# A two-layer state-space and expert kernel: the norm of the chunk two ahead begun in round 17 for 20, x loaded in six pieces, idle products at the start, first repeats in another order, and the last image's normalised tiles kept on chip

## The chip, the cores and the metric

The kernel runs on one core of one Trainium2 chip. The metric is the device time of one execution in microseconds (us). It was taken in five runs; one further view is a profile of one of these executions, from which every row below comes. The engines are named as the profile names them: PE (TensorE, matmuls; PEld is its weight loads), DVE (VectorE), ACT (ScalarE), POOL (GpSimd) and SP (SyncE, which issues nearly all DMAs). All arithmetic is in 32-bit floats, for which the profile records two passes for each matmul instruction.

## The reference

`x` has 8 images of 384 channels and 32 x 32 points, which are 1024 tokens an image. Two layers follow one another, each of the form `x = x + layer(group_norm(x))` with 32 groups that span a whole image.

```
# layer 0: a state-space block and an MLP
t = layernorm(tokens(gn(x))) * ln_w + ln_b
xm, z = split(t @ in_proj.T)                     # 768 + 768
xc = silu(causal_conv3(xm) + conv_b)
dt, B, C = split(xc @ x_proj.T)                  # 24, 16, 16
dt = softplus(dt @ dt_proj.T + dt_b)
h[l] = exp(dt[l]*A) * h[l-1] + dt[l]*xc[l]*B[l]  # 768 channels x 16 states, over 1024 tokens
y = (sum over states of h[l]*C[l] + xc*D) * silu(z)
t = y @ out_proj.T
x = x + gelu(t @ mlp_w1.T + b1) @ mlp_w2.T + b2
# layer 1: four experts, all computed, weighted
g = gn(x); scores = softmax(g @ gate_w + gate_b); the top 2 of 4 give coefficients
x = x + sum over e of coef[e] * (relu(g @ w1[e].T + b1[e]) @ w2[e].T + b2[e])
```

The coefficients of an expert are switched on by whether any token of the whole batch has picked it, so the expert sums wait for the scores of all images.

## The kernel before, in words

**Tiling.** Channels lie on the 128 partitions and tokens in the free dimension. A chunk `i` is half an image, T = 512 tokens; there are NCH = 16 chunks, two an image (NH = 2). A tile `xt` is 128 x 3 x 512. The 768 inner channels are six blocks `d`; the 16 states are four groups `s` of four. One (chunk, block, group) is a round `r`, so a chunk has 24 rounds and the kernel 384. In a round 32 channels times 4 states lie on the partitions, four quarters `j` long: quarters 0 and 1 are the half A, quarters 2 and 3 the half BB.

**A round.** POOL's `drive` (L813) multiplies the repeated `dt*xc` (tile `dxr`) with B into `du`, 128 x 2048 elements. ACT makes four decays `exp(dt*A)` (L805, from the tiles `dtr_a` and `dtr_b`), DVE runs four scans along the tokens (L821) and multiplies the half A with C (L825), POOL does that for the half BB (L825), and PE adds the states up with eight passes of a selecting matrix into `y` (L847).

**What feeds a round.** `delta(i, d)` makes dt of a block: a product on PE (L444), three activations on ACT (L448 to L452), a maximum on DVE (L454); it then writes dt to DRAM, multiplies dt with xc on POOL (L460), writes that too (`written`, L430), and reads both back repeated over the states (`repeat`, L436): two loads into `dtr_b`, four into `dxr`, two into `dtr_a`, 256 KB each.

**What runs beside the rounds.** Norm, in_proj with convolution and gates of the next chunk; out_proj, both MLP products and the expert hidden layers (`e_hid`, L677) of earlier chunks. The weights of these four come in 192 KB blocks through a `Stream` each, which keeps two blocks ahead (L237). A block of products is three matmul instructions of 128 x 512, six passes. The expert hidden tiles `r` go to DRAM.

**The order.** All engines' instructions are put out by a planner in the kernel (`run`, L983): the rounds are chains of steps with fixed costs per step, the rest are tasks (generators) that yield the engine and the cost of their next step and have a rank; the planner fills tasks into what its own clock takes for gaps. The order in which instructions stand on each engine, SP's DMAs included, is therefore fixed when the kernel is built; on the chip each engine takes them in that order. `plan(i, k)` (L1003) begins tasks in round k of chunk i, among them at k == 20 the norm of chunk i + 2; the convolutions of chunk i + 2 begin at k == 4 of chunk i + 1. `norm` (L279) needs the group statistics of the image, which `statistics` (L252) takes from six further loads of x, begun at k == 3 of the first chunk of the image before.

**The start.** Two loads of x (768 KB each), then statistics, norm, convolutions, x_proj and `delta(0, 0)` of chunk 0, each run to its end; then the first B and C rows, `delta(0, 1)`, three gates, the norm of chunk 1, the first two blocks of each of the four weight streams, and the rounds.

**The end.** After the last round PE still has out_proj and MLP of chunk 15 and what is left of the experts. The group statistics of layer 1's last image are complete only with the last MLP product of chunk 15; then `scores` (L622) normalises chunks 14 and 15 in place in the tile `x1`, writes each to DRAM (`xn_dram`, L631), makes the gate scores (L635, L645), and the expert lane reads each back (`load_xn`, L660) before its 12 blocks of `e_hid`. At the moment of the last MLP product, `second_layers` (L1099) has its first loads put out: two `r` tiles, the second expert weights (2304 KB), a bias and an `x1` tile. `route` makes the coefficients. Then 1152 passes of the second expert products follow (L1169).

Of the kernel before, what the change touches and what calls it, by code (L numbers as in the profile page):

```python
# [27 lines left out]
Q = 4  # L28
# [12 lines left out]
LAG = 0.07  # L41
SLACK = {"DVE": 0.35, "ACT": 0.15, "POOL": 0.3}
BATCH_SLACK = 0.5
SHORT = 0.5
RANK = 16.0
POLL = 0.5
# [75 lines left out]
def layers(ctx, tc, io, ident, cmean, eps, dram, x1_dram, gn1, logits, r_dram, group_norm):  # L122
# [25 lines left out]

    def load_x(i):
        xt[i] = pxt.tile([P, J, T], F32, name="xt")  # L150
        nc.sync.dma_start(xt[i], chunk_of(io["x"], i))

    for i in range(NH):
        load_x(i)
# [283 lines left out]
    def delta(i, d):  # L438
        while i not in dbc or making_dt:
            yield "-", POLL  # L440
        making_dt.append((i, d))
        yield "bank", MM
        g = bank("g_dt")
        PE.matmul(g, lhsT=w_dt[:, d * P:(d + 1) * P], rhs=dbc[i][0:DTR, :], start=True, stop=True)  # L444
        yield "ACT", ACT
        projected.add((i, d))
        dt = p1.tile([P, T], F32, name="dt")
        S.activation(dt, g, AF.Relu, bias=b16[:, d:d + 1], scale=-1.0)  # L448
        yield "ACT", ACT
        S.activation(dt, dt, AF.Exp, bias=top, scale=-1.0)  # L450
        yield "ACT", COPY
        S.activation(dt, dt, AF.Ln, bias=1.0)  # L452
        yield "DVE", DVE
        V.scalar_tensor_tensor(dt, g, b_dt[:, d:d + 1], dt, ALU.add, ALU.max)  # L454
        yield "-", 0
        free()
        there = written("dtr", i, d, dt)
        yield "POOL", MULT
        dtx = p1.tile([P, T], F32, name="dtx")
        G.tensor_tensor(dtx, dt, xc[i, d], ALU.mult)  # L460
        yield "-", 0
        there_x = written("dxr", i, d, dtx)
        yield "-", DMA
        making_dt.clear()
        last = i * per + d * NG - 1
        while issued["B"] < last - NG:
            yield "-", POLL
        dtr[i, d] = {}
        pair = pdt.tile([P, 2, T], F32, name="dtr_b")
        for k in range(2):  # L470
            repeat(pair[:, k, :], there, 2 + k)
        yield "-", 0
        while issued["drive"] < last - NG:
            yield "-", POLL
        dtr[i, d]["B"] = pair
# [24 lines left out]
    def out_proj(i):  # L500
        while (i, ND - 1) not in finished or i - 1 in tt:
            yield "-", POLL
        t = p1.tile([P, J, T], F32, name="tt")
        for j in range(J):
            g = None
            for k in range(2):
                yield "bank" if k == 0 else "PE", 3 * MM
                w = w_out.take("out_proj", 2 * j + k)
                g = bank("g_out") if k == 0 else g
                for d in range(3):  # L510
                    PE.matmul(g, lhsT=w[:, d, :], rhs=xc[i, 3 * k + d], start=(k + d == 0), stop=(k == 1 and d == 2))  # L511

            current[0].holds -= 1
            begin(evict(g, COPY, "ACT", lambda g, j=j: S.copy(t[:, j, :], g),
                        lambda j=j: ready.setdefault(i, []).append(j)), rank=1, after=now[0] + 3 * MM, holds=1)
        yield "-", 0
        out_done.add(i)
        while len(ready.get(i, [])) < J:
            yield "-", POLL
        tt[i] = t  # L520

    def hidden(i, us):
        while i not in tt:
            yield "-", POLL
        for u in us:
            while len(waiting) == HID:
                yield "-", POLL
            yield "bank", 3 * MM
            waiting.add((i, u))
            w = w_1.take("mlp_w1", u)  # L530
            g = bank("hid")
            for j in range(J):
                PE.matmul(g, lhsT=w[:, j, :], rhs=tt[i][:, j, :], start=(j == 0), stop=(j == J - 1))  # L533

            def then(g, u=u):
                h = pre[i, u] = ph.tile([P, T], F32, name="h")
                S.activation(h, g, AF.Identity, bias=b1[:, u:u + 1])
            current[0].holds -= 1
            begin(evict(g, ACT, "ACT", then), rank=1, after=now[0] + 3 * MM, holds=1)
            if u % 3 == 2:  # L540
                begin(gelus(i, range(u - 2, u + 1)))
# [20 lines left out]
    def second(i, half):  # L562
        us = range(half * NF // 2, (half + 1) * NF // 2)
        for j in range(J):
            g = None
            for k in range(2):
                mine = [(i, us[3 * k + n]) for n in range(3)]
                while not all(m in hs for m in mine) or i not in x1:
                    yield "-", POLL
                yield "bank" if k == 0 else "PE", 3 * MM  # L570
                w = w_2.take("mlp_w2", 4 * j + 2 * half + k)
# [50 lines left out]
    def scores(b):  # L622
        yield from group_norm(stats.pop(b), bank, free, p2, gn1[b])
        for i in range(b * NH, (b + 1) * NH):
# [2 lines left out]
                yield "ACT", 0.8  # L627
                S.activation(xn[:, j, :], xn[:, j, :], AF.Identity, bias=gn1[b][:, 1:2], scale=gn1[b][:, 0:1])
            yield "-", 0
            xn_dram[i] = dram.tile([P, J, T], F32, name=f"xn_dram{i}")  # L630
            nc.sync.dma_start(xn_dram[i], xn)  # L631
            yield "bank", 1.1
            g = bank("g_logits")
            for j in range(J):
# [18 lines left out]

    xns, xn_dram = {}, {}

    def load_xn(i, pool):
        while i not in scored:
            yield "-", POLL
        xn = pool.tile([P, J, T], F32, name="xn")
        nc.sync.dma_start(xn, xn_dram[i])  # L660
        yield "-", 2 * DMA
        xns[i] = xn
# [1 line left out]
    def expert_lane():  # L664

        for i in range(NCH):
            if i < NCH - 1:
                yield from load_xn(i, pxn)
            while i not in xns:
                yield "-", POLL  # L670
            xn = xns.pop(i)
            for u in range(E * J):
                yield "bank", 3 * MM
                w = w_e.take("e_w1", u)
                h = bank("e_hid")
                for j in range(J):
                    PE.matmul(h, lhsT=w[:, j, :], rhs=xn[:, j, :], start=(j == 0), stop=(j == J - 1))  # L677
# [131 lines left out]
    def drive(r):  # L809
        i, d, s = at(r)  # L810
        issued["drive"] = r
        du[r] = pdu.tile([P, Q, T], F32, name="du")
        G.tensor_tensor(du[r], dxr[i, d], wide(bt[i, s].unsqueeze(1), [P, Q, T]), ALU.mult)  # L813

    def scan(r, j):
# [187 lines left out]
    def plan(i, k):  # L1003
# [8 lines left out]
        if n < NCH:  # L1012
# [11 lines left out]
                begin(delta(n, 0), rank=0)  # L1024
            if k == 20:
                begin(delta(n, 1), rank=0)
        if k == 20 and n + 1 < NCH:
            begin(norm(n + 1), rank=1)
        if k == 3 and i + NH < NCH:
            begin(next_x(i))  # L1030
# [68 lines left out]
    def second_layers():  # L1099
# [37 lines left out]
        e2 = weight("e_w2", [P, E, J, J, P])  # L1137
        eb2 = weight("e_b2", [P, E, J])
        load_sum(0)
        begin(load_xn(NCH - 1, we), route(we), rank=0)  # L1140
        run(lambda: routed)
        load_coef(0)
        run(everything)
# [19 lines left out]
        for n, (i, e) in enumerate(todo):  # L1163
# [10 lines left out]
            if e == E - 1:  # L1174
                expert_out(i, acc)

    with tc.manual_schedule():
        w_in = Stream(pw_in, [("in_proj", k) for k in in_order()])
        begin(statistics(0))
        run(everything)  # L1180
        begin(norm(0))
        run(everything)
# [9 lines left out]
        for s in range(1, NG):  # L1192
# [3 lines left out]
        begin(*(gate(0, d) for d in range(3)))  # L1196
        begin(silus(zs, gates, [(0, d) for d in range(3)]))
        begin(norm(1))
        w_out = Stream(pw_out, [("out_proj", k) for i in range(NCH) for k in range(2 * J)])
        w_1 = Stream(pw_1, [("mlp_w1", u) for i in range(NCH) for u in range(NF)])  # L1200
        w_2 = Stream(pw_2, [("mlp_w2", 4 * j + 2 * half + k) for i in range(NCH) for half in range(2)
                            for j in range(J) for k in range(2)])
        seed(0, 0)
        w_e = Stream(pw_e, [("e_w1", u) for i in range(NCH) for u in range(E * J)])
        begin(out_lane(), rank=1.5)
        begin(hidden_lane(), rank=3)
        begin(second_lane(), rank=2.5)
        begin(expert_lane(), rank=4)
        scan_chains()
        run(lambda: summed.get(NCH - 1) == J)  # L1210
        scanning.close()
# [42 lines left out]
```

## Time and profile before

| | us |
|---|---|
| five runs, median (lowest to highest) | 3817.44 (3816.41 to 3820.63) |
| the profiled execution, its own time | 3820.63 |
| its span, first to last instruction | 3818.9 |
| first drive on POOL to last sum of states on PE | 71.1 to 3126.2 |
| second expert products on PE | 3319.0 to 3813.4 |

| engine | busy us | share of span |
|---|---|---|
| PE | 3584.6 | 94% |
| DVE | 3022.5 | 79% |
| POOL | 2773.2 | 73% |
| ACT | 2377.1 | 62% |

Matmuls are pipelined and a waiting one counts as busy, so PE's share says less than it seems to. A chunk takes 183 to 197 us, read from the starts of POOL's drives.

### The profile page before, as it was taken

How to read it: one execution, taken by the hardware profiler on the slowest of the kernel's cores; microseconds unless marked ns; L12 is line 12 of the kernel's file. 1: busy time of each engine (PE TensorE's matmuls, PEld its weight loads, DVE VectorE, ACT ScalarE, POOL GpSimd, SP SyncE). 2: the span in 40 equal slices, each digit the busy share in tenths (PEclk: the TensorE clock that was granted, in tenths of full speed). 3: DMA queues.
4: the chain of work that ended last, by engine and by line, in shares of the span. 5: the costliest groups of instructions: out<-in, count | busy, mean ns of one | idle time of the engine just before them, and what ended most of it. 6: DMA issues, size and time to landing. Idle time of an engine off the chain costs nothing.

```text
span 3818.9 us, 35175 instructions
## 1 busy us (share of the span) xinstructions
PE 3584.6 (94%) x10294; PEld 1367.2 (36%) x10294; DVE 3022.5 (79%) x3097; ACT 2377.1 (62%) x3714; POOL 2773.2 (73%) x1070
## 2 busy tenths in 40 slices
PE   6769798999999999999999999999999998999999
PEld 2213232333333333333333333333333333444444
DVE  3988989899889998989888898988898870355554
ACT  4758677868687878687867687778776843100000
POOL 2898989989989988899888988998899960000000
PEclk8869899999999999999999999999999999999999
DMA  4334455565656665655565655555555543655553
GB/s 134 125 121 150 151 164 170 173 203 176 194 176 201 203 202 178 198 183 196 181 200 172 198 180 193 186 194 180 200 168 200 182 157 133 230 190 189 182 185 107
DMA packets 374804, 677.90 MB, mean 178 GB/s; under 512 B 40508, under 2 KB 151484, under 8 KB 372436
## 3 DMA queue, kind: packets, MB, share of 16 engines
q1 hardware_dynamic: 372448, 675.31, 53.4%
q8 instruction: 83, 1.36, 0.2%
q14 instruction: 109, 0.89, 0.1%
q10 hardware_dynamic: 2164, 0.34, 0.1%
HBM read 535.90 MB, written 139.59 MB: 177 GB/s over the span
## 4 chain that ended last, share of the span: by engine, by line
PE 52%; DVE 15%; ACT 13%; POOL 8%; DMA 6%; issue 5%; SPq 2%; ACTq 0%; POOLq 0%; DVEq 0%
PE acc L1169 13%; PE e_hid L677 8%; PE acc L574 7%; PE hid L533 7%; DVE da_A L821 6%; PE g_in L325 6%; POOL du L813 5%; PE y L847 5%; DVE du L821 4%; ACT da_A L805 4%; PE g_out L511 3%; DVE du L825 2%; POOL du L825 2%; ACT da_B L805 2%; ACT L205 1%
## 5 line engine op out<-in xcount | busy, mean ns | idle before, releaser
L813 POOL TENSOR_TENSOR du<-dxr,b 128x2048 f32<-128x2048 f32 x384 | 1738.6, 4535 | 84.9 <-PE y L847 54.5
L825 POOL TENSOR_TENSOR du<-du,c 128x1024 f32<-128x1024 f32 x384 | 905.2, 2358 | 130.8 <-DVE du L821 91.6
L805 ACT ACTIVATE da_A<-dtr_a,w_a_log 128x512 f32<-128x512 f32 x768 | 529.5, 689 | 284.9 <-DVE du L825 103.8
L805 ACT ACTIVATE da_B<-dtr_b,w_a_log 128x512 f32<-128x512 f32 x768 | 526.0, 685 | 250.0 <-DVE du L821 236.1
L325 PE MATMUL g_in<-xt,in_proj 128*128 128x512 f32 x1152 | 550.6, 620 | 26.9 <-DMA in_proj<-in_in_proj 12.5
L677 PE MATMUL e_hid<-xn,e_w 128*128 128x512 f32 x1152 | 535.7, 607 | 25.9 <-DMA e_w<-in_e_w 18.8
L574 PE MATMUL acc<-h,mlp_w 128*128 128x512 f32 x1152 | 538.2, 606 | 15.4 <-DMA mlp_w<-in_mlp_w 8.7
L821 DVE TENSOR_TENSOR_SCAN du<-da_B,carry,du 128x512 f32<-128x512 f32 x384 | 487.5, 1270 | 82.3 <-ACT da_B L805 68.5
L821 DVE TENSOR_TENSOR_SCAN da_A<-da_A,carry,du 128x512 f32<-128x512 f32 x384 | 491.2, 1279 | 68.7 <-ACT da_A L805 63.5
L847 PE MATMUL y<-du,sel 128*32 128x512 f32 x3072 | 461.7, 623 | 88.9 <-POOL du L825 36.5
L533 PE MATMUL hid<-tt,mlp_w 128*128 128x512 f32 x1152 | 525.3, 601 | 14.5 <-DMA mlp_w<-in_mlp_w 5.1
L821 DVE TENSOR_TENSOR_SCAN du<-da_B,du 128x512 f32<-128x512 f32 x384 | 464.5, 1210 | 81.7 <-ACT da_B L805 45.4
L821 DVE TENSOR_TENSOR_SCAN da_A<-da_A,du 128x512 f32<-128x512 f32 x384 | 467.7, 1218 | 50.0 <-ACT da_A L805 42.6
L1169 PE MATMUL acc<-r,w_e_w 128*128 128x512 f32 x1152 | 494.6, 592 | 0.0
L825 DVE TENSOR_TENSOR du<-da_A,c 128x1024 f32<-128x1024 f32 x384 | 467.8, 1218 | 9.2
L325 PEld LDWEIGHTS g_in<-xt,in_proj 128*128 128x128 f32 x1152 | 216.9, 196 | 351.9 <-issue 266.0
L677 PEld LDWEIGHTS e_hid<-xn,e_w 128*128 128x128 f32 x1152 | 216.6, 193 | 321.4 <-issue 266.0
L574 PEld LDWEIGHTS acc<-h,mlp_w 128*128 128x128 f32 x1152 | 212.5, 191 | 325.6 <-issue 262.6
L533 PEld LDWEIGHTS hid<-tt,mlp_w 128*128 128x128 f32 x1152 | 213.4, 191 | 309.4 <-issue 250.3
L1169 PEld LDWEIGHTS acc<-r,w_e_w 128*128 128x128 f32 x1152 | 219.4, 190 | 275.0 <-issue 275.0
L511 PE MATMUL g_out<-xc,out_proj 128*128 128x512 f32 x576 | 272.6, 611 | 3.7 <-DMA out_proj<-in_out_proj 3.5
L847 PEld LDWEIGHTS y<-du,sel 128*32 128x32 f32 x3072 | 69.4, 110 | 417.1 <-issue 97.8
(126 smaller groups left out, 2962.8 us busy)
## 6 DMA issues: line engine op xcount, KB each, us to landing
dxr<-dxr_dram SPq DMA_DIRECT2D x384, 256.0 KB, 4.7
mlp_w<-in_mlp_w SPq DMA_DIRECT2D x384, 192.0 KB, 3.8
dtr_b<-dtr_dram SPq DMA_DIRECT2D x192, 256.0 KB, 4.1
dtr_a<-dtr_dram SPq DMA_DIRECT2D x192, 256.0 KB, 3.3
r_dram<-r SPq DMA_DIRECT2D x192, 256.0 KB, 3.5
r<-r_dram SPq DMA_DIRECT2D x64, 768.0 KB, 4.7
in_proj<-in_in_proj SPq DMA_DIRECT2D x192, 192.0 KB, 3.8
e_w<-in_e_w SPq DMA_DIRECT2D x192, 192.0 KB, 3.8
```

The lines of the kernel that those rows point to most:

```text
L205: S.preload_act_table_set(EXP_LN_SET)
L325: PE.matmul(g, lhsT=w[:, j, :], rhs=xt[i][:, j, :], start=(j == 0), stop=(j == J - 1))
L511: PE.matmul(g, lhsT=w[:, d, :], rhs=xc[i, 3 * k + d], start=(k + d == 0), stop=(k == 1 and d == 2))
L533: PE.matmul(g, lhsT=w[:, j, :], rhs=tt[i][:, j, :], start=(j == 0), stop=(j == J - 1))
L574: PE.matmul(g, lhsT=w[:, n, :], rhs=hs[mine[n]], start=(k + n == 0), stop=(k == 1 and n == 2))
L677: PE.matmul(h, lhsT=w[:, j, :], rhs=xn[:, j, :], start=(j == 0), stop=(j == J - 1))
L805: S.activation(out, dtr[i, d][pair][:, j % 2, :], AF.Exp, scale=neg_a[:, d, j, s:s + 1])
L813: G.tensor_tensor(du[r], dxr[i, d], wide(bt[i, s].unsqueeze(1), [P, Q, T]), ALU.mult)
L821: V.tensor_tensor_scan(a if j < 2 else b, a, b, start, ALU.mult, ALU.add)
L825: engine.tensor_tensor(du[r][:, js, :], h, wide(ct[i, s].unsqueeze(1), [P, 2, T]), ALU.mult)
L847: PE.matmul(y[j * m:(j + 1) * m, :], lhsT=sel, rhs=h[:, j, :], start=False, stop=(s == NG - 1), tile_position=(0, j * m), skip_group_check ...
L1169: PE.matmul(acc[j], lhsT=e2[:, e, d, j, :], rhs=r[:, d, :], start=(e + d == 0), stop=(e + d == E + J - 2))
```

## The change

Six edits, in the order of the program.

1. `load_x` loads a tile of x in three pieces of 256 KB, for all chunks.
2. For the very first block (i + d == 0) `delta` multiplies dt with xc on DVE instead of POOL, and reads the repeats back in another order: one piece of `dtr_b`, two of `dxr`, one of `dtr_a`, two of `dxr`, then the second pieces of `dtr_b` and `dtr_a`. The first round's drive is done in two halves, BB on DVE and A on POOL.
3. `IDLE` = 24 products of the identity matrix with itself, 128 columns each, are put out beside the first statistics.
4. The four weight streams and their lanes begin when round 4's half A has been read out, instead of before the rounds.
5. The norm of chunk i + 2 begins at k == 17 instead of 20.
6. The normalised tiles of the last image stay in `x1`: no write to DRAM and no reload; the expert products read them there. The second half of the expert blocks of chunk 13 is held back until the last MLP product.

```diff
-        nc.sync.dma_start(xt[i], chunk_of(io["x"], i))
+        for j in range(J):
+            nc.sync.dma_start(xt[i][:, j, :], chunk_of(io["x"], i)[:, j, :])
...
-        yield "POOL", MULT
+        if i + d == 0:
+            yield "DVE", DVE
+        else:
+            yield "POOL", MULT
         dtx = p1.tile([P, T], F32, name="dtx")
-        G.tensor_tensor(dtx, dt, xc[i, d], ALU.mult)
+        (G if i + d else V).tensor_tensor(dtx, dt, xc[i, d], ALU.mult)
...
+        if i + d == 0:
+            b, a = pdt.tile([P, 2, T], F32, name="dtr_b"), p1.tile([P, 2, T], F32, name="dtr_a")
+            x4 = pdt.tile([P, Q, T], F32, name="dxr")
+            repeat(b[:, 0, :], there, 2)
+            for j in (2, 3):
+                repeat(x4[:, j, :], there_x, j)
+            repeat(a[:, 0, :], there, 0)
+            for j in (0, 1):
+                repeat(x4[:, j, :], there_x, j)
+            repeat(b[:, 1, :], there, 3)
+            repeat(a[:, 1, :], there, 1)
+            dtr[i, d], dxr[i, d] = {"A": a, "B": b}, x4
+            return
...
-            xn_dram[i] = dram.tile([P, J, T], F32, name=f"xn_dram{i}")
-            nc.sync.dma_start(xn_dram[i], xn)
+            if i < NCH - NH:
+                xn_dram[i] = dram.tile([P, J, T], F32, name=f"xn_dram{i}")
+                nc.sync.dma_start(xn_dram[i], xn)
...
-            if i < NCH - 1:
-                yield from load_xn(i, pxn)
-            while i not in xns:
+            if i < NCH - NH:
+                yield from load_xn(i)
+            while i not in scored:
                 yield "-", POLL
-            xn = xns.pop(i)
+            xn = xns.pop(i) if i < NCH - NH else x1[i]
             for u in range(E * J):
+                while i == NCH - NH - 1 and u >= E * J // 2 and summed.get(NCH - 1) != J:
+                    yield "-", POLL
...
+        if r == 0:
+            V.tensor_tensor(du[r][:, BB, :], dxr[i, d][:, BB, :], wide(bt[i, s].unsqueeze(1), [P, 2, T]), ALU.mult)
+            G.tensor_tensor(du[r][:, A, :], dxr[i, d][:, A, :], wide(bt[i, s].unsqueeze(1), [P, 2, T]), ALU.mult)
+            return
...
-        if k == 20 and n + 1 < NCH:
+        if k == 17 and n + 1 < NCH:
             begin(norm(n + 1), rank=1)
...
-        begin(load_xn(NCH - 1, we), route(we), rank=0)
+        begin(route(we), rank=0)
...
+    def lanes():
+        while ("A", NG, 4) not in ends:
+            yield "-", 10 * POLL
+        w_out = Stream(pw_out, [("out_proj", k) for i in range(NCH) for k in range(2 * J)])
...
+    def idle_products():
+        yield "bank", 0.2
+        g = bank("idle")
+        for k in range(IDLE):
+            PE.matmul(g[:, 0:P], lhsT=ident, rhs=ident, start=True, stop=True)
+        yield "-", 0
+        free()
...
-        begin(statistics(0))
+        begin(statistics(0), idle_products())
...
-        w_out = Stream(pw_out, [("out_proj", k) for i in range(NCH) for k in range(2 * J)])
...
-        begin(expert_lane(), rank=4)
+        begin(lanes())
         scan_chains()
```

More of the change, by code (lines that the diff above doesn't have):

```diff
@@ L43 @@
 BATCH_SLACK = 0.5
+IDLE = 24
 SHORT = 0.5
@@ L457, in delta @@
         there = written("dtr", i, d, dt)
-        yield "POOL", MULT
+        if i + d == 0:
+            yield "DVE", DVE
+        else:
+            yield "POOL", MULT
         dtx = p1.tile([P, T], F32, name="dtx")
-        G.tensor_tensor(dtx, dt, xc[i, d], ALU.mult)
+        (G if i + d else V).tensor_tensor(dtx, dt, xc[i, d], ALU.mult)
         yield "-", 0
         there_x = written("dxr", i, d, dtx)
-        yield "-", DMA
+        yield "-", DMA if i + d else 0
         making_dt.clear()
+        if i + d == 0:
[11 more added lines that the diff above has]
+            return
         last = i * per + d * NG - 1
@@ L507, in out_proj @@
                 yield "bank" if k == 0 else "PE", 3 * MM
-                w = w_out.take("out_proj", 2 * j + k)
+                w = streams["out_proj"].take("out_proj", 2 * j + k)
                 g = bank("g_out") if k == 0 else g
@@ L529, in hidden @@
             waiting.add((i, u))
-            w = w_1.take("mlp_w1", u)
+            w = streams["mlp_w1"].take("mlp_w1", u)
             g = bank("hid")
@@ L570, in second @@
                 yield "bank" if k == 0 else "PE", 3 * MM
-                w = w_2.take("mlp_w2", 4 * j + 2 * half + k)
+                w = streams["mlp_w2"].take("mlp_w2", 4 * j + 2 * half + k)
                 g = bank("acc") if k == 0 else g
@@ L654, in layers, with load_xn @@
     xns, xn_dram = {}, {}
-    def load_xn(i, pool):
+    def load_xn(i):
         while i not in scored:
             yield "-", POLL
-        xn = pool.tile([P, J, T], F32, name="xn")
+        xn = pxn.tile([P, J, T], F32, name="xn")
         nc.sync.dma_start(xn, xn_dram[i])
@@ L666, in expert_lane @@
         for i in range(NCH):
-            if i < NCH - 1:
-                yield from load_xn(i, pxn)
-            while i not in xns:
+            if i < NCH - NH:
+                yield from load_xn(i)
+            while i not in scored:
                 yield "-", POLL
-            xn = xns.pop(i)
+            xn = xns.pop(i) if i < NCH - NH else x1[i]
             for u in range(E * J):
+                while i == NCH - NH - 1 and u >= E * J // 2 and summed.get(NCH - 1) != J:
+                    yield "-", POLL
                 yield "bank", 3 * MM
-                w = w_e.take("e_w1", u)
+                w = streams["e_w1"].take("e_w1", u)
                 h = bank("e_hid")
@@ L1175, in second_layers @@
                 expert_out(i, acc)
+    streams = {}
+    def lanes():
+        while ("A", NG, 4) not in ends:
+            yield "-", 10 * POLL
+        w_out = Stream(pw_out, [("out_proj", k) for i in range(NCH) for k in range(2 * J)])
+        w_1 = Stream(pw_1, [("mlp_w1", u) for i in range(NCH) for u in range(NF)])
+        w_2 = Stream(pw_2, [("mlp_w2", 4 * j + 2 * half + k) for i in range(NCH) for half in range(2)
+                            for j in range(J) for k in range(2)])
+        w_e = Stream(pw_e, [("e_w1", u) for i in range(NCH) for u in range(E * J)])
+        streams.update(out_proj=w_out, mlp_w1=w_1, mlp_w2=w_2, e_w1=w_e)
+        begin(out_lane(), rank=1.5)
+        begin(hidden_lane(), rank=3)
+        begin(second_lane(), rank=2.5)
+        begin(expert_lane(), rank=4)
+    def idle_products():
[5 more added lines that the diff above has]
+        free()
     with tc.manual_schedule():
         w_in = Stream(pw_in, [("in_proj", k) for k in in_order()])
-        begin(statistics(0))
+        begin(statistics(0), idle_products())
         run(everything)
@@ L1198, in layers @@
         begin(norm(1))
-        w_out = Stream(pw_out, [("out_proj", k) for i in range(NCH) for k in range(2 * J)])
-        w_1 = Stream(pw_1, [("mlp_w1", u) for i in range(NCH) for u in range(NF)])
-        w_2 = Stream(pw_2, [("mlp_w2", 4 * j + 2 * half + k) for i in range(NCH) for half in range(2)
-                            for j in range(J) for k in range(2)])
         seed(0, 0)
[L1204 to L1207, printed above, removed]
-        begin(expert_lane(), rank=4)
+        begin(lanes())
         scan_chains()
```

## The prediction

> **What bounds the kernel now.** I read the page's slices first, then the chain of waits at both ends, the transfers, and the order in which the changed kernel's instructions stand on each engine.
>
> ```profile
> PE   6769798999999999999999999999999998999999
> PEclk8869899999999999999999999999999999999999
> L813 POOL TENSOR_TENSOR du<-dxr,b 128x2048 f32<-128x2048 f32 x384 | 1738.6, 4535 | 84.9 <-PE y L847 54.5
> L825 POOL TENSOR_TENSOR du<-du,c 128x1024 f32<-128x1024 f32 x384 | 905.2, 2358 | 130.8 <-DVE du L821 91.6
> ```
>
> The slices show PE full from the fourth on, with a lower clock before. The POOL groups give the floor of a round: 4.54 + 2.36 = 6.9 us, while 384 rounds from 71.1 to 3126.2 average 7.95. So three stages have different limits: a serial start, rounds a little above POOL's floor with PE nearly full, and a tail in which PE alone counts.
>
> The chain of waits at the start (start us, us, what):
>
> ```profile
> 60.51 2.64 DMA dtr_dram<-dt
> ...
> 69.56 6.18 DMA b<-bc_dram
> 75.75 6.34 DMA mlp_w<-in_mlp_w
> 82.15 4.43 DMA dxr_dram<-dtx
> ...
> 92.13 1.13 ACT z L379 x2
> ```
>
> The end of it:
>
> ```profile
> 3231.85 2.23 ACT x L628 x3
> 3234.08 0.02 issue
> 3234.10 11.66 DMA xn_dram<-x
> 3245.76 0.02 issue
> 3245.77 5.62 DMA xn<-xn_dram
> 3251.39 0.04 issue
> 3251.43 16.12 PE e_hid L677 x30
> ```
>
> After the last MLP product (PE ends it at 3227.2) nothing runs on PE but small products until 3251.4. Why the write takes 11.66 us is seen in the transfers issued from 3227.5 to 3234 (KB each, us to landing):
>
> ```profile
> w_e_w<-in_e_w SPq DMA_DIRECT2D x1, 2304.0 KB, 12.1
> x<-x_dram SPq DMA_DIRECT2D x1, 768.0 KB, 12.6
> w_e_b<-in_e_b SPq DMA_DIRECT2D x1, 6.0 KB, 11.6
> ```
>
> A load of 6 KB, issued at 3230.6, lands after 11.6 us: SP's queue delivers in the order of issue, and the bulk of the second expert stage stands ahead.
>
> **x in six pieces, and what waits behind.** Before, DVE stops after two statistics at 6.9 for the bias load w_conv_b (landed 8.2), and ends with gn_mv at 11.5. The order view puts that copy behind the fourth statistic, and three small reductions behind gn_mv. x's last byte landed at 7.8; two statistics at 0.65 and the aggregation then end near 9.4. Gain at most 2.3. The four extra issues at the start cost SP 0.6 each, beside transfers that need until 7.8 anyway; later ones (two more a chunk) stand in an SP queue whose next loads are issued blocks ahead: nothing, or 1.2 us a chunk if that lead is gone, which no row shows.
>
> **Idle products.** They stand ahead of gn_m on PE, 48 passes from 1.5 (the identity's last POOL step). No row has this shape. The nearest is the 96x4 product (L645): 0.126 a pass at full clock (12.1/96), 0.234 at half clock (1.87/8 at 3236.7, granted clock 0.50). If the 128 columns hide under the weight load, half the passes at each rate give 8.6 us, so an end at 10.1; all at the fast rate 7.5. If columns (0.107 or 0.213, a quarter of a 512-column pass) come on top and the clock stays half, 48 x 0.447 = 21.5, an end at 23.0. I take 10.1, as the large products hide their weight loads. gn_m then starts at 10.1 instead of 11.7: 1.6 gained, between 2.3 and minus 11.3.
>
> Do they make the norm's products faster? The window view of the clock (PE busy (x), PEld, DVE, ACT, POOL, PEclk, DMA share, GB/s):
>
> ```profile
> 21.50:28.30 6.80, 5.49 (x6) 1.80 (x6) 0.00 (x0) 2.55 (x4) 0.00 (x0) 0.51 0.00 0
> 3231.00:3251.00 20.00, 10.39 (x28) 4.65 (x28) 4.46 (x12) 7.02 (x14) 0.00 (x0) 0.50 0.90 333
> ```
>
> PE had paused 2.8 us (19.5 to 22.3) before the first stretch and ran at half clock in it. Between the end of the idle products and `mu` lie some 3.4 us with three one-column products, so I count no gain; if the clock held, `mu` would take 2.6 for 4.2 and 1.6 more came off. [...]
>
> **First repeats, first drive.** POOL's dtx (1.27) becomes 0.7 on DVE, and the 4.54 drive becomes 1.2 on DVE and 2.36 on POOL. Before, the eight repeats landed 65.9 to 72.3, about 0.7 apart. The halves of `dxr` now come second, third, fifth and sixth, so the drive could end near 73. But the order view still has DVE's dt of block 1 ahead of the first scan; its activations stand on ACT behind both decays of half A, and the second needs the last piece of `dtr_a`, again eighth of eight. Before: last landing 72.3, ACT's Ln until 75.05, dt 75.14, first scan 75.81, with the drive done at 75.6. So I count nothing; 3 us if dt were not there.
>
> **Streams begun after round 4.** In the old order eight loads of 192 KB stand between the C rows (last landed 79.6) and the in_proj block that PE waits for (landed 84.07); PE's gate product starts at 84.20, its copy closes the gates' SiLU batch, and the decay behind that batch ends DVE's wait of 6.26 us at 95.95. The eight took 79.6 to 83.5, so 3.9 come off that wait, which leaves 2.4. They move behind the repeats of block 2; SP issued nothing from 115 to 129 there, and they need 4, so the cover is 14 us; without it the dtr write of block 3 would be 4 later. Gain 3.9, between 0 (that cover gone) and 6.3.
>
> **The norm in round 17.** The order view shows mu at rounds 16 or 17 instead of 19 or 20 in the seven odd chunks from 1 to 13; in the even ones the image's statistics come at rounds 21 to 23 in both kernels and hold it there. The next convolutions stand at rounds 4 to 6 either way. So nothing that waited for the norm comes earlier; 3.6 us of DVE (two operations of 1.79) and some 5.4 of ACT move three rounds ahead. Its six passes of mu and var each move on PE past `acc` and `hid` blocks, its loads not at all. Odd chunks before: rounds 20 to 22 take 6.4, 6.9 and 7.3 us (POOL's floor), rounds 15 to 17 take 9.8, 9.6 and 8.9 (waits), round 23 takes 9.4. I take 0, nearest to what total work says: PE, DVE, ACT and POOL have the same instructions. The ends: 7 x 3.6 = 25 lost if DVE's part lengthens rounds that were late already, 7 x 2.5 = 17.5 gained if round 23 falls to the floor.
>
> **The last image.** A block is six passes of 0.429 (494.41 us / 1152 in the last stage) = 2.575. After the last sum (3126.2) the order view has 31 expert blocks for 32, and the six held blocks after the last MLP product.
> - Up to the last MLP product: 1 + 30 blocks = 79.8, the old 2.7 wait for GELU, and 0.6 for the last `tt` copy, which an expert block used to cover: 83.1, for 101.0 before.
> - Then two held blocks run on weights already loaded (5.2). The third's weight load is issued behind the bulk, whose last tile landed 16.7 us after PE's end; 0.5 for its own bytes makes 17.2. PE idles about 12.
> - Then 28 blocks = 72.1, both chunks' scores 4.1 (12.6/12 and 12.1/12 us a chunk, beside idle PE before, now between blocks), 0.7 for small products, 3.2 for a half clock at restart (16.12 for 30 passes before, 12.9 at full clock), 1.9 for the wait behind the 1024 KB `spread` load, as before: 82.0.
>
> Sum 182.3, for 192.8 (3126.2 to 3319.0): 10.5 gained. If the third weight block came at once, 12 + 3 more; if the restart found all six queued transfers 5 later, 5 less. [...]
>
> **Sum.** 1.6 + 3.9 + 10.5 = 16.0. The profiled execution took 3820.6 (span 3818.9 plus 1.7 around it), 3.2 above the median of 3817.4; so 3804.6 against it, 3801.4 against the median.
>
> **The rivals.** About 0.2%, 7.6 us, is what a measurement of this kernel can tell from no change: 3809.8 and 3825.1.
> - *The rounds gain too*: round 23 of the odd chunks falls to the floor, 3801.4 - 17.5 = 3784. For: those rounds are waits. Against: ACT's and DVE's long waits there end on other tasks as well.
> - *Idle products outlast the statistics*: at 0.447 a pass gn_m starts 11.3 late; 3801.4 + 1.6 + 11.3 = 3814, no change that shows. For: no row shows 128 columns behind a fresh weight load at half clock. Against: the large products hide theirs.
> - *Slower: the norm lands on late rounds.* DVE's 3.6 us lengthen rounds 16 to 19 of seven odd chunks: 3801.4 + 25 = 3826. It decides from 3.4 us an odd chunk on, when 16 gained are spent and 7.6 more. For: those rounds wait already, and rounds 20 to 22 at the floor can give nothing back. Against: a wait there is filled as well as lengthened.
>
> **How the numbers follow.** My sum with its steps' ends (3791 to 3811): 0.61, of which 0.06 fall above 3809.8. The rounds gain: 0.13. Idle products outlast: 0.12. Norm on late rounds: 0.14. So faster 0.55 + 0.13 = 0.68, same 0.06 + 0.12 = 0.18, slower 0.14. The range takes in 3784 and 3826, with 2 beyond each for the spread of the runs: 3782 to 3828; the likeliest case alone is 3791 to 3811.
>
> **What would show it.** First gn_m near 10 and idle products ended by then; first scan still near 74; DVE's wait ahead of the third round near 2.4; chunks of 183 to 197 us as before; PE idle about 12 us after two held blocks, ended by a weight load, and no `xn_dram` for chunks 14 and 15; last sum to second expert products near 182. I am wrong if chunks move by more than 2 us each on average, or if the held blocks run through.

## The result and the profile after

The changed kernel took 3817.9 us in the median of 25 runs, the kernel before 3820.2 in 45 runs beside it: a ratio of 0.9994, 95% interval 0.9989 to 1.0. That is 2.3 us, within the 0.2% that tells nothing from no change; I had forecast 16. The profiled execution took 3816.1, its span is 3814.4.

The page's slices and POOL groups of the changed kernel (busy tenths; then busy us and mean ns, then idle before and what ended most of it):

```profile
PE   7769898999999999999999999999899998999999
PEclk8869899999999999999999999999999999999999
L841 POOL TENSOR_TENSOR du<-dxr,b 128x2048 f32<-128x2048 f32 x383 | 1734.4, 4534 | 94.5 <-PE y L875 69.7
L853 POOL TENSOR_TENSOR du<-du,c 128x1024 f32<-128x1024 f32 x384 | 905.0, 2357 | 128.5 <-DVE du L849 97.5
```

One drive fewer has this shape, as it was split; the others cost what they did. What grew is POOL's wait for `y`, the sums on PE (54.5 before).

The chain at the end (start us, us, what), with the two stops that I forecast:

```profile
3216.24 2.59 PE e_hid L701 x6
...
3220.78 13.03 DMA e_w<-in_e_w
...
3233.85 7.90 PE e_hid L701 x12
...
3277.55 6.00 DMA e_w<-in_e_w
...
3283.68 31.14 PE e_hid L701 x72
```

Nothing waits for `xn_dram` any more, and PE stops for the third held block's weights: 12.1 us of waiting for a load that took 13.0.

From the profiles I read three stretches. The start ends at chunk 1's first scan, the rounds end at the last y sum on PE, and the tail ends at the first of the second expert products. I later profiled the changed kernel twice more; its column is the mean of three.

| stretch, us | before | after | change | forecast |
|---|---|---|---|---|
| start: to chunk 1's first scan | 265.2 | 259.4 | -5.8 | -5.5 |
| rounds: from there to the last y | 2861.0 | 2870.8 (2870.9, 2874.6, 2867.0) | +9.8 | 0 |
| tail: to the second expert products | 192.7 | 183.3 | -9.4 | -10.5 |

Both ends moved as forecast. The rounds gave most of it back. One expert block only changed places: 31 stand behind the last y for 32 before, so the rounds hold 967 passes of `e_hid` for 961. At 2.6 us a block, that much of the tail's gain and of the rounds' loss is this block.

### The profile page after: what moved, and what is told of

The parts are those of the page before. It is cut to its first block, busy times and chain, and to the rows that moved or that the text cites. A ratio compares the mean times of both kernels' runs of the same rounds, so it can differ in the third digit from the quotient of the medians.

```text
span 3814.4 us, 35318 instructions
## 1 busy us (share of the span) xinstructions
PE 3595.2 (94%) x10342; PEld 1376.9 (36%) x10342; DVE 3024.4 (79%) x3099; ACT 2380.4 (62%) x3714; POOL 2770.3 (73%) x1069
## 4 chain that ended last, share of the span: by engine, by line
PE 52%; DVE 10%; ACT 8%; POOL 6%; DMA 5%; issue 4%; SPq 1%; POOLq 0%; ACTq 0%; DVEq 0%
PE acc L1197 13%; PE e_hid L701 8%; PE hid L552 7%; PE acc L593 7%; PE g_in L327 6%; PE y L875 4%; DVE da_A L849 4%; POOL du L841 4%; PE g_out L530 4%; DVE du L849 3%; ACT da_A L829 3%; POOL du L853 1%; DMA e_w<-in_e_w 1%; DVE du L853 1%; PE g_dt L446 1%
## 5 line engine op out<-in xcount | busy, mean ns | idle before, releaser
L593 PE MATMUL acc<-h,mlp_w 128*128 128x512 f32 x1152 | 548.9, 616 | 22.7 <-ACT h L568 11.1
L701 PE MATMUL e_hid<-xn,e_w 128*128 128x512 f32 x1008 | 477.0, 614 | 45.5 <-DMA e_w<-in_e_w 34.9
L701 PEld LDWEIGHTS e_hid<-xn,e_w 128*128 128x128 f32 x1008 | 190.6, 195 | 311.5 <-issue 231.4
L715 ACT ACTIVATE r<-e_hid,w_e_b 128x512 f32<-128x512 f32 x192 | 129.8, 680 | 176.2 <-PE e_hid L701 118.9
```

The costliest lines, as they stand in the source:

```text
L715: S.activation(r, h, AF.Relu, bias=e_b1[:, u:u + 1])
```

## Experiments

After the change 311 of the 384 rounds hold other PE work than before, from round 16 of chunk 1 on. Without the move of the norm, only the very first round differs. So the rounds could be tested apart from the rest. My theory was that the new order of the rounds cost the 10 us; the rivals were that the earlier start or the later streams cost it, or that it was spread.

**One part at a time.** The norm alone (and, the other way round, all but the norm):

```
-        if k == 20 and n + 1 < NCH:
+        if k == 17 and n + 1 < NCH:
             begin(norm(n + 1), rank=1)
```

> The kernel before with one edit: the norm of the next chunk begins in round 17 instead of 20. Theory (the new order of the rounds is what gave the gains back; the two profiles have 2870.9 us from chunk 1's first scan to the last y sum, against 2861.0): start and tail as before (first scan near 75.8, last y to second expert products near 193), the stretch from chunk 1's first scan to the last y longer by about 10 us, time about 10 us above the kernel before. Rival 1 (the middle lost because the earlier start and the later weight streams shifted everything): no change, within 3 us. Rival 2 (both orders are equal and the profiled difference is spread between executions): no change either, and the stretch within 3 us of 2861.

> The changed kernel with the norm begun in round 20 again, all else of the change kept. Theory (start and tail add, the norm's order was what cost): 4.5 + 9.6 = 14 us faster than the kernel before, with the stretch from chunk 1's first scan to the last y back near 2861. Rival 1 (the start's shift is what costs): as the changed kernel, 2 to 4 us faster than before, with the stretch near 2871.

The four edits of the start alone, then the tail's (held blocks, no `xn_dram` for chunks 14 and 15) alone:

> The kernel before with the edits of the start alone: x in six pieces, idle products, first repeats and first drive, streams begun after round 4. From chunk 0's second round on every engine has the same order as before. Theory: chunk 1's first scan near 260.5 (265.2 before), the rest as before, so 4 to 5 us faster. Rival 1 (the start's shift costs in the rounds what it brings): chunk 1 begins near 260.5, but the stretch from there to the last y grows by 5 to 10 us, and the time is the same or up to 5 us slower.

> The kernel before with the last image's edit alone: six expert blocks held back until the last y sum, chunks 14 and 15 kept on chip. The rounds' order is as before. Theory: last y to second expert products 183 us instead of 193, so 9 to 10 us faster, with PE idle for about 12 us on the third held block's weights. Rival (the blocks held back and the writes left out slow or speed the rounds of the last chunk): the stretch up to the last y moves by more than 3 us, and the time with it.

| kernel | median us | ratio to before, 95% | rounds | tail |
|---|---|---|---|---|
| norm alone | 3849.1 | 1.0084 (1.0070 to 1.0097) | 2876.9 | 204.0 |
| start alone | 3818.0 | 0.9997 (0.9988 to 1.0006) | 2864.2 | 193.1 |
| tail alone | 3815.4 | 0.9985 (0.9977 to 0.9994) | 2857.4 | 185.6 |
| all but the norm | 3809.5 | 0.9979 (0.9970 to 0.9988) | 2860.6 | 186.5 |

With the norm back in round 20 the rounds are back at 2860.6, and the time is 8.4 below the changed kernel's. So the move of the norm is what cost, and the start's shift costs the rounds nothing that shows. The parts brought less than I expected of each: the start alone 1.1 us for 4 to 5 (interval from 4.6 gained to 2.3 lost), the tail alone 5.7 for 9 to 10 (2.3 to 8.8), both together 8.0 for 14 (4.6 to 11.5). The start's stretch moved as expected (259.3), the tail's by 7.1. The norm alone missed my figure: 29 us for 10. Its order leaves six expert blocks more behind the last y (38 for 32), 15 us of PE's work, of which 11 show in the tail, and the rounds still grew by 16. The same edit of one number thus cost 29 in one kernel and 8 in the other: with the changed start the planner puts out another order from chunk 3 on.

**Is it the norm's place, or any new order?** Here, with the norm in round 20, no instruction and no task's begin differs; the planner is told another cost for one activation of the image norm, and so reorders the rounds from chunk 5, or chunk 3, on:

```
-                yield "ACT", 0.8
+                yield "ACT", 0.9
                 S.activation(xn[:, j, :], xn[:, j, :], AF.Identity, ...)
```

The second kernel is told 0.7. A third run keeps the figure and begins the norm in round 18.

> The changed kernel with the norm in round 20, and the planner told 0.9 us instead of 0.8 for one activation of the image norm; no instruction differs, only the order, from chunk 5 on. Theory A (any new order of the rounds costs or gains some us by accident, and the move of the norm cost so): the time moves away from the 3809.5 of the run with round 20, by the six expert blocks more that stand after the last y sum (37 for 32, and one MLP block more) 15 us slower, and up to 15 more or less in the rounds. Theory B (moving the norm earlier is what costs, by its place ahead of late work; an order without that move costs nothing): within 4 us of 3809.5.

> As the run before, with 0.7 us instead of 0.8: another order from chunk 3 on, with 30 expert blocks after the last y sum. Theory A: away from 3809.5 by some us in either direction, 5 us faster by the two blocks fewer if its rounds are as long. Theory B: within 4 us of 3809.5.

> The changed kernel with the norm in round 18 instead of 17. Theory A (order by accident): anywhere between 3800 and 3840. Theory B (the earlier the norm, the more it costs; 17 cost 8.4 us against 20): two thirds of that, so 5.6 above 3809.5, near 3815, and the stretch from chunk 1's first scan to the last y near 2867.

The same two figures with the norm in round 17:

> The changed kernel (norm in round 17) with the planner told 0.9 us instead of 0.8 for one activation: another order from chunk 3 on, no instruction differs. Theory (what costs is any order other than that of the kernel before, wherever the norm stands; orders with the norm in 20 but a figure changed took 3846 and 3849): between 3815 and 3855, with the stretch from chunk 1's first scan to the last y over 2868. Rival (the norm in 17 costs its own 8 us on top of what a changed figure costs, 37): 3850 to 3860.

> As the run before with 0.7 us instead of 0.8: a third order with the norm in round 17. Theory: between 3815 and 3855, stretch over 2868. Rival (the norm's own 8 on top of 39): 3853 to 3863.

| norm begun in round | figure told | median us | against 3809.5 | blocks after the last y |
|---|---|---|---|---|
| 20 | 0.8 | 3809.5 | 0 | 32 |
| 20 | 0.9 | 3846.1 | +36.6 | 37 |
| 20 | 0.7 | 3849.0 | +39.5 | 30 |
| 18 | 0.8 | 3818.1 | +8.6 | 30 |
| 17 | 0.8 (the change) | 3817.9 | +8.4 | 31 |
| 17 | 0.9 | 3827.6 | +18.1 | 32 |
| 17 | 0.7 | 3812.7 | +3.2 | 33 |

All seven are built with the same start and tail, but for the blocks left over. A norm in 17 can cost 3, which is too little to tell from nothing (0.9984, 0.9976 to 0.9993, for the first row's 0.9979, 0.9970 to 0.9988); a norm left in 20 can cost 40. The rival that the move adds a fixed 8 to what a changed figure costs wanted 3850 to 3863 for the last two rows; they took 3827.6 and 3812.7. So the move has no fixed price, and giving up the old order can cost far more than the norm's instructions; none of the six other orders was faster. That the move as such is free does not follow. Round 18 does not decide: its rounds of 2869.7 and its 3818.1 are near the rival's 2867 and 3815. My own ranges missed as well. I had expected at most 30 lost for the figure 0.9, and for the last row over 3815 and rounds over 2868; its rounds took 2862.5. My expectation for the 0.7 kernel with the norm in 20, 5 us faster for its two blocks fewer if its rounds kept their length, missed by the rounds: 2915.0, 54 longer. The count of blocks left over, which can be read before a run, is no guide.

**In what form an order loses.** The windows over the rounds, first with the norm in round 20, then the changed kernel (stretch, its length, busy us and instructions of PE, PEld, DVE, ACT and POOL, granted clock, DMA share, GB/s):

```profile
260.30:3120.90 2860.60, 2746.25 (x8344) 1018.81 (x8343) 2552.59 (x2540) 2174.98 (x3387) 2591.90 (x977) 0.98 0.56 184
```

```profile
260.70:3131.60 2870.90, 2757.38 (x8349) 1026.71 (x8347) 2551.71 (x2540) 2177.62 (x3389) 2592.06 (x977) 0.98 0.56 183
```

PE is idle for 114.4 us in the one and 113.5 in the other. The loss of 10 lies in PE's busy time. The block more is some 2.6 of it, by its own time; the other matmuls are the same. DVE and POOL took what they took: the steps that moved cost nothing more in themselves. The timeline of PE in the changed kernel shows how busy time grows:

```profile
1184.08 1.06 PE L875 MATMUL y<-du,sel 128*32 128x512 f32 x8
1188.84 5.46 PE L701 MATMUL e_hid<-xn,e_w 128*128 128x512 f32 x6 [3.69 <-DMA e_w<-in_e_w]
```

```profile
1188.70:1194.30 5.60, 5.46 (x7) 2.39 (x8) 4.59 (x4) 2.86 (x5) 5.17 (x2) 0.50 0.91 304
```

After a pause of 3.69 for weights the granted clock is 0.50, and six passes take 5.46 us for 2.58 at full clock. The pause cost 3.7 and 2.9 behind it. The trace's clock records give each such stretch with its length, so the rounds can be split for every profile: PE's pauses; half of PE's busy time at half clock; and the rest, which is the work at full clock.

| us in the rounds | length | pauses | lost to the clock | rest | stretches at half clock |
|---|---|---|---|---|---|
| old order, mean of eight profiles | 2861.4 (2857.4 to 2867.1) | 115.8 | 38.3 (33.6 to 43.8) | 2707 | 14 to 17 |
| changed kernel, mean of three | 2870.8 (2867.0 to 2874.6) | 116.1 | 47.9 (46.0 to 51.4) | 2707 | 20 to 22 |
| norm in 17, figure 0.7, two | 2860.8 | 114.8 | 35.9 | 2710 | 15 and 17 |
| norm in 17, figure 0.9 | 2887.4 | 125.0 | 51.8 | 2711 | 24 |
| norm in 20, figure 0.7 | 2915.0 | 144.8 | 55.6 | 2715 | 24 |
| norm in 20, figure 0.9 | 2881.7 | 127.8 | 54.1 | 2700 | 20 |
| norm in 18 | 2869.7 | 118.1 | 37.9 | 2714 | 17 |
| norm in 17, start and tail of before | 2876.9 | 137.3 | 46.2 | 2693 | 21 |

The rest differs by 2.6 for each expert block that stands in the rounds and not behind them; differences of up to some 7 us remain beside that.

Four of these profiles were taken to tell this from spread:

> The changed kernel profiled again. If the loss is in the granted clock: stretch from chunk 1's first scan to the last y near 2870, PE pauses 112 to 119 in it, clock loss over 43. If that was spread: stretch near 2870 with pauses over 120 and clock loss under 41.

> As the run before, a third profile of the changed kernel: stretch near 2870, pauses 112 to 119, clock loss over 43 if the loss is in the clock.

> The kernel with the norm in round 20 profiled again: stretch 2857 to 2867, pauses 112 to 119, clock loss 32 to 41, as in the seven profiles with the old order so far.

> The order with the norm in round 17 that lost least (3812.7) profiled again: stretch near 2862, pauses 112 to 119 and clock loss 32 to 41, like the old order, if pauses and clock are what sets an order's time.

These expectations count the clock loss by windows of 10 us, which gave 48 in the first profile of the change; the two repeats gave 42.1 and 41.8, just under the 43 set, with 32.4 for round 20 and 33.1 and 32.2 for the figure 0.7. The pauses came to 120.9 and 114.0. By the records' own lengths, in the table, all three profiles of the change stand above all eight of the old order. So the changed kernel loses 9.6 to the clock and 0.3 to pauses, of 9.4. The split is good to a few us only: for the block more the rest should have grown by 2.6, and it did not. The slowest order loses both ways. Round 18, in the one profile of it, of its fastest execution (3812.2), loses nothing to the clock; its rounds are longer by two blocks and 2.3 of pauses.

**Where the clock is lost.** The seven odd chunks from 1 to 13 are those in which the norm moved. Their rounds 20 to 23, which it left, read as follows before and in the changed kernel (columns as in the windows above; chunk 13, then the sums over the seven chunks):

```profile
2725.12:2760.13 35.01, 33.43 (x99) 12.72 (x97) 32.55 (x31) 25.41 (x39) 34.19 (x11) 1.00 0.67 223
sum 233.74, PE 217.08 PEld 80.93 DVE 221.57 ACT 158.74 POOL 222.78; mean PE 31.01 PEld 11.56 DVE 31.65 ACT 22.68 POOL 31.83
```

```profile
2726.20:2761.45 35.25, 27.47 (x73) 10.15 (x72) 27.30 (x24) 24.98 (x38) 27.99 (x9) 0.90 0.63 209
sum 230.83, PE 198.92 PEld 72.97 DVE 198.82 ACT 159.63 POOL 204.57; mean PE 28.42 PEld 10.42 DVE 28.40 ACT 22.80 POOL 29.22
```

PE pauses here for 31.9 us instead of 16.7, and loses 12.7 to the clock instead of 0.2. In all profiles it is 29.8 to 33.7 of pauses with 12.2 to 12.7 lost in the changed kernel, and 15.7 to 18.3 with 0.2 to 2.7 in the old order. In rounds 16 to 19, where the norm now stands, the pauses fell from 10.4 to 2.9 and the loss from 2.2 to nothing. Everywhere else the loss is 34.9 in the old order and 35.5 in the changed kernel. So the added loss stands at the place that the norm left, where other work replaced its products only in part. Pauses of 29 to 35 us stand there in all five orders with the norm in 17 or 18, so they come with the move; of the two new orders with the norm in 20 one has 15.1 and one 28.1. They do not fix the price: the five orders lose 3.0 (figure 0.7) to 15.1 us (figure 0.9) to the clock there. No run filled these pauses, so that the loss follows from them is read from the traces and not tested.

What PE waits for shifted too. The waits of PE in the rounds (us in all, times, longest), with the norm in round 20, in the changed kernel, and with the figure 0.7 and the norm in round 20:

```profile
PE y L875 <- DVE du L853: 21.9, 13, 5.7
PE e_hid L701 <- DMA e_w<-in_e_w: 16.2, 6, 4.0
```

```profile
PE e_hid L701 <- DMA e_w<-in_e_w: 22.8, 13, 4.2
PE y L875 <- DVE du L853: 10.4, 9, 4.6
```

```profile
PE e_hid L701 <- DMA e_w<-in_e_w: 27.7, 11, 5.7
PE acc L593 <- DMA mlp_w<-in_mlp_w: 20.5, 13, 6.5
```

The old order pauses ahead of the sums. The changed kernel pauses for weights. The wait for `e_w` is longer in all seven other orders, 17.6 to 31.2 us for 13.5 to 16.9 in the old one; the shortest belongs to the figure 0.7 with the norm in 17, which lost next to nothing. Whether a deeper ring of weight blocks would heal it was not tried.

**The start.** The streams alone:

> The kernel before with the four weight streams begun after round 4, and nothing else; same order in every round. Theory (this part alone gives the start's gain): gn_m near 12 and first scan near 76 as before, DVE's wait ahead of the third round from 6.3 to under 1.5, chunk 1's first scan 5 earlier, time 1 to 5 us faster than before. Rival (x, the idle products or the first repeats bring part of it): wait still over 3 us, chunk 1's first scan less than 3 earlier.

3815.2 us, 0.9994 (0.9986 to 1.0003), which cannot be told from no change; chunk 1's first scan at 261.6. The third round's wait is gone here (0.25 us), as in the changed kernel, where it was 6.26 before (timeline of DVE):

```profile
91.45 1.22 DVE L849 TENSOR_TENSOR_SCAN du<-da_B,du 128x512 f32<-128x512 f32 x1 [0.43 <-ACT da_B L829]
```

First scan to chunk 1's first scan is 184.0 with the streams alone, 183.4 to 183.5 with all four edits, 189.4 before. So the streams bring nearly all of it. Why x and the idle products brought next to nothing stands in ACT's timeline of the changed kernel; PE has gn_m from 10.44 to 10.79:

```profile
11.31 0.61 ACTq L184 DMA_DIRECT2D gate_b<-in_gate_b  x1
11.96 0.28 ACT L185 ACTIVATE w_a_log<-w_a_log 128x96 f32<-128x96 f32 x1 [9.88 <-DMA w_e_b<-in_e_b]
12.15 0.15 ACT L104 ACTIVATE gn_gm<-gn_m 128x1 f32<-128x1 f32 x1
```

ACT issues the small weight loads until 11.9, and reads gn_m only then; before, it read it at 12.30.

**A version that beats both.** First the bulk loads of the second expert stage are issued one by one beside the held blocks, in the kernel with the norm in round 20:

```
-        e2 = weight("e_w2", [P, E, J, J, P])
+        def bulk():
+            for e in range(E):
+                nc.sync.dma_start(e2[:, e], io["e_w2"][:, e])
+                yield "-", 5.0
+            # then the chunk's sum and two r tiles, 5.0 apart
+        begin(bulk(), rank=0)
```

> The changed kernel with the norm in round 20, and the bulk loads of the second expert stage no longer issued at once ahead of the held blocks: the four parts of the weights, the chunk's sum and its first two hidden blocks are issued one by one, about 5 us apart. The order of every round is as in the kernel before. Theory (PE's idle of 12 us in the tail is SP's queue delivering in order): the wait for the third held block's weights falls from 12 to under 3, the last y to second expert products from 186 to 176, time near 3800, 10 below the run with round 20. Rival (the transfers share the same engines, and the waits come back block by block): the tail stays within 3 us of 186.

3797.0 us, 0.9942 (0.9928 to 0.9955); tail 173.3. PE's waits in the tail, first of the changed kernel, then of this one:

```profile
PE e_hid L701 <- DMA e_w<-in_e_w: 13.4, 2, 12.1
```

```profile
PE e_hid L701 <- DMA e_w<-in_e_w: 3.3, 2, 2.1
```

Then two things at once: five small weight loads go from ACT's queue to SP's, and four idle products follow gn_m, five gn_v:

> The kernel of the run with the bulk loads spread, with two edits at the start: five small weight loads move from ACT's queue to SP's (in the changed kernel gn_m ended at 10.8 but ACT issued loads until 11.9 and read it at 12.15), and nine more idle products stand behind gn_m and gn_v, so that PE pauses less than 2 us ahead of mu. Theory: ACT reads gn_m at once, near 11; mu takes under 3.5 us instead of 5.1; first scan 3 us earlier, near 73.3; the time 3 us lower than 3797, near 3794. Rival (the clock stays down whatever the pause, or SP's loads delay in_proj): mu over 4.5, first scan over 75.

3787.9 us, 0.9921 (0.9909 to 0.9934): 9 below the run before, where I expected 3. The start accounts for 5.3 (chunk 1's first scan at 254.4 for 259.8); the rounds, in the old order in both, took 2861.4 and 2867.1 in the two profiles, which is its spread. ACT reads gn_m at 10.65, the first scan is at 71.1 for 76.3, and PE at the start reads:

```profile
1.53 7.99 PE L1250 MATMUL idle<-ident 128*128 128x128 f32 x48 [1.53 <-POOL ident masks.py:199]
13.18 2.84 PE L301 MATMUL mu<-xt,mean_w 128*128 128x512 f32 x6
18.80 4.17 PE L318 MATMUL var<-sq,cmean 128*128 128x512 f32 x6 [2.78 <-ACT sq L314]
```

With the pauses filled, `mu` takes 2.84, near the 2.58 of six passes at full clock, for 5.47 in the changed kernel and 4.35 before. A pause of 2.78 later, `var` takes 4.17.

## Why the prediction was wrong

**The step that failed** is "I take 0, nearest to what total work says" for the norm in round 17. The order view had shown me that the rounds held other work, and I priced only the norm's own instructions. The term measured +9.4 (2870.8 for 2861.4), of which some 2.6 is the expert block that I had counted as gained in the tail and not as added to the rounds. The argument, same instructions and so same time, fails on PE's own account: the rest of 2707 us is the same, but pauses and the clock take 154 us of these rounds in the old order, 164 in the new one, and up to 200 in another. What the argument leaves out is the place that the norm leaves: rounds 20 to 23 of the odd chunks lose 12.4 to the clock for 1.2. My sign of being wrong showed it too: from first scan to first scan, chunks 1 to 14 moved by 3.7 to 4.2 us each on average, up or down, for 0.8 to 1.2 among profiles of the old order.

**The ends of that term** were drawn from the norm as well. The slower rival, DVE's 3.6 us on late rounds, had the wrong place and mechanism: rounds 16 to 19 of the odd chunks took 217.1 us before and 212.4 after. The faster one saw its condition come true and got nothing for it: by POOL's drives, round 23 of the odd chunks fell from 9.0 us to 6.7 (my 9.4 left out chunk 1), while round 18 rose from 7.9 to 10.0 and round 22 from 8.1 to 10.4. Orders with the norm unmoved lost 37 and 40, so bounds from the norm's own work were too narrow for an edit that rewrites 311 rounds.

**x in six pieces, idle products.** gn_m came at 10.4 for the 10.1 forecast; the idle products took 8.0 us for 8.6 and ended at 9.5, so gn_m waited for the statistics and not for them. But the 1.6 were not gained, since ACT's issues stood behind; I had followed DVE and SP, not ACT's queue. No gain for `mu` was right (5.47 for 4.35, even 1.1 lost), and the reason given, the pause behind the idle products, agrees with the run in which it was filled.

**First repeats.** Nothing, as forecast: first scans at 74.9 to 77.1 in the three profiles, 75.8 before.

**Streams.** 3.9 forecast; the wait fell by 5.8, from 6.26 to 0.43, and that is the start's gain.

**The last image.** Right: 183.3 for 182.3, with the forecast stop of 12 us, though 2.6 of the 10.5 was the block that moved into the rounds. The block's weights landed 13.0 after their issue, behind the bulk, and with the bulk spread the wait is 2.1; all transfers that SP issued from 3217 to 3222 landed in the order of issue: the bulk's 2304 KB 12.1 after their issue, 6 KB issued 0.75 behind them after 11.5. The case of a third block that comes at once, 12 + 3 us more gained, did not happen.

**The sum.** Start and tail alone would be the 3809.5 of the kernel with the norm in 20: 0.9979, 8.0 us (4.6 to 11.5) under the kernel before. Its stretches give more, 4.9 and 6.2 of start and tail against the one profile of before; its 32 blocks for 31 cost it 2.6 of the tail forecast. Some 3 us between profiles and runs are left unassigned. The rival nearest to the measured time, idle products that outlast the statistics (3814), did not happen, as they ended before; the two others are answered above.

**Still open**: why pauses end at half clock in one order and not in another, as in rounds 20 to 23 with the figures 0.8 and 0.7. The changed kernel has no more pauses over 2.8 us than the old order (11 in each profile, 9 to 12 in the old order) and five or six stretches more at half clock.

## What to carry to other kernels

Where a planner writes the order, an edit of one begin time, or of one cost figure, is a new order everywhere behind it: price it by what other orders took, not by the moved step, and hold the old order when another part is to be measured. Ask also what fills the busiest engine's pauses at the place that a step leaves. Split the busiest engine's time into work, pauses and clock loss before saying that equal work takes equal time; a pause of 3.7 us here cost 2.9 more behind it. At a serial start, follow the next reader's whole queue, its DMA issues too, before counting an earlier producer as gained.

## What was not expected of the hardware

All stretches at reduced clock that begin in the rounds stand at 0.50 in the clock records: 16 in the profile of the kernel before, 22 in the first of the changed kernel. They last 3.41 us (9 and 11 of them), or two, three or, once in the kernel before, five times that (17.07). By the table, 38 us of 2861 to 56 of 2915 were lost to the clock in the rounds, 1.3% to 1.9%. In the changed kernel half clock also followed a pause of 2.05 us, PE being busy for 0.95 of the 3.0 us up to 378.5:

```profile
377.69 4.54 PE L593 MATMUL acc<-h,mlp_w 128*128 128x512 f32 x6 [2.05 <-ACT h L568]
```

Its six passes took 4.54 instead of 2.58, with 0.50 granted from 378.5 to 381.9. An identity product of 128 columns in 32-bit floats took 0.166 us a pass (7.96/48, in the changed kernel), less than a pass of 512 columns at either clock: 0.43 (2.58/6) at full, 0.91 (5.46/6) at half.
